# Four attention projections as 64x64 tiles in one round beside the scores, in a kernel of eight fused blocks

## The chip, the cores and the metric

The kernel is one program on one core of a Trainium2 chip. The time is device time in microseconds from launch to end, and each kernel is run several times. Five engines work from queues of their own, each in program order: TensorE (PE, with its weight loads shown apart as PEld), VectorE (DVE), ScalarE (ACT), GpSimd (POOL), and SyncE (SP), which issues DMAs. They wait for each other through semaphores.

## The reference

The input is 4096 tokens of 128 numbers. Four layers follow each other, each an attention block and a feed-forward block, each on the layer norm of what came before and added to it. The change lies in the last part, where layer 2 and layer 3 are computed together. Layer 2's attention has 16 heads of 64 numbers over sequences that the kernel treats in batches of 512 tokens:

```
def _L2_attn_ref(x, q_w, q_b, k_w, k_b, v_w, v_b, l_w, l_b):
    q = jnp.einsum('bsd,hpd->bhsp', x, q_w) + q_b
    k = jnp.einsum('bsd,hpd->bhsp', x, k_w) + k_b
    v = jnp.einsum('bsd,hpd->bhsp', x, v_w) + v_b
    scores = jnp.einsum('bhqp,bhkp->bhqk', q, k) / jnp.sqrt(jnp.float32(P))
    attn = jax.nn.softmax(scores, axis=2)
    ctx = jnp.einsum('bhqk,bhkp->bqhp', attn, v)
    out = concat @ l_w.T + l_b
```

The softmax runs over the queries (axis 2), so that each key has its own maximum and sum. Its four projections are q, k, v and the output projection with l_w. Layer 2's feed-forward is a mixture of experts on the first 1024 tokens. Layer 3's first block is a product with W1 plus a causal filter of 20 taps followed by a product with W2; its second block quantizes its inputs to a 4-bit grid in blocks of 16, takes a gate and an up product (352 wide), multiplies silu(gate) by up, quantizes again, and takes the down product.

## The kernel before

All tokens stay on the chip as eight tiles x[b] of 128 partitions by 4 x 128 (a batch b of 512 tokens). Layers 0 and 1 come first and are not touched by the diff. The function `late` (from L1386) does layers 2 and 3. Its main loop (L2140) has N = 64 *frames*, one for each batch b and pair of heads cc (n = 8 b + cc). The order on every engine is written out by hand: the program is recorded with a manual schedule, and each engine executes its instructions in the order in which the Python code emits them. A frame emits:

- `scores(n, 0)` (L1494): for two of the four key tiles, four products of 64 rows by 64 columns by 512, which use the four quarters of the PE array, into a buffer of two banks (`bank2`, two buffers); DVE takes the maxima (L1514), ACT the exponentials with sums (L1520).
- the hook "P", called between the exponentials of the two key tiles, then the hook "V".
- `context(n-1)` (L1542): sixteen records of 128 rows by 64 columns by 512, into the bank "c", copied to `ct` by ACT (L1555).
- `weigh(n, 0)` (L1530), which divides the values by the sums on DVE and POOL, and the hook "G".
- `scores(n, 1)` for the other two key tiles.
- `queries(n+2)` (L1482): two products of 128x128 by 512, to `pk` and `pq`; ACT evacuates q (L1490), DVE k (L1491).
- `output(n-1, ct)` (L1558): four products by token, `ct` as weights, l_w moving, 128 columns each, accumulated over the eight frames of a batch in the bank "o"; after the eighth DVE adds it to x[b] (L270).
- `values(n+1)` (L1465): four products by token into the bank "c"; DVE evacuates v (L1480).
- `weigh(n, 1)` and the hook "E".

The products are float32; each call of `mm` (L246) leaves two load and two matmul records in the trace. `bank()` without a name gives one of two buffers of one bank in turn ("one"), which queries share with everything that the hooks compute on PE.

Everything else is hung into the frames by a table: `at(frame, hook, f)` (L1404). The layer norm that prepares layer 2's input of batch b (`norm_steps`, L1412: `stats` on DVE and POOL, `scale` on ACT, `turn_`, four PE transposes and a copy by ACT) is hung in from frame 8 b - 10 (L1934). Two batches go through the experts after frames 9 and 17 (L1588). Layer 3 of batch b starts at frame 8 b + 8, or 8 b + 9 for b < 2 (L1940), and `planned` (L1884) hangs its steps into the frames after that: norm, filter taps on DVE (`conv_v`) and on ACT with POOL (`conv_s`), `conv_out` (two products and the addition), a second norm, `quant_x1`/`quant_x2`, `turn_x`, four times `gated` (gate and up on PE, tanh on ACT) with `gated_v` on DVE, `quant_h1`/`quant_h2`, `turn_h` and `down`. For b > 0 three of the four gated products stand in hook "E", and the queries of those frames are emitted earlier, between the second scores' exponentials (`early_q`). Layer 3 of the last batch, and the end of the one before it, are written out in `end` (L1961).

Of the kernel before, what the change touches and what calls it, by code (L numbers as in the profile page):

```python
# [17 lines left out]
F32 = mybir.dt.float32  # L18
I32 = mybir.dt.int32
U32 = mybir.dt.uint32  # L20
AF = mybir.ActivationFunctionType
ALU = mybir.AluOpType
AX = mybir.AxisListType

P = 128
D = 128
NB = 8
# [133 lines left out]
def body(ctx, tc, dram, spans, x_in, ib, it, ic, ei, out):  # L161
# [110 lines left out]
    def cols(t, j):  # L272
        return t[:, j * P : (j + 1) * P]
# [1112 lines left out]
    def late():  # L1386
# [11 lines left out]
        with tc.tile_pool(name="a2", bufs=2) as wp, tc.tile_pool(name="l3", bufs=1) as lp:  # L1398
            N = NB * 8
            qb = wp.tile([P, 8], F32, tag="qb", name="qb", bufs=1)  # L1400
            xts, vs_, qks, exs, outs = {}, {}, {}, {}, {}
            steps = {}

            def at(frame, hook, *fs):  # L1404
# [60 lines left out]
            def values(n):  # L1465
                if n < N:
                    b, cc = divmod(n, 8)
                    ps = bank("c")
                    pv = ps.rearrange("p (j n) -> p j n", j=J)
                    for j in range(J):  # L1470
                        mm(
                            pv[:, j, :],
                            cols(xts[b], j),
                            cols(a2["v"], cc),
                            start=(j == 0),
                            stop=(j == J - 1),
                        )
                    vs_[n] = v = wp.tile([P, J, P], F32, tag="v", name="v")
                    bias = cols(bc["vb"], cc).unsqueeze(1).to_broadcast([P, J, P])
                    nc.vector.tensor_tensor(v, pv, bias, ALU.add)  # L1480

            def queries(n):  # L1482
                if n < N:
                    b, cc = divmod(n, 8)
                    pk, pq = bank(), bank()
                    mm(pk, cols(a2["k"], cc), xts[b])
                    mm(pq, cols(a2["q"], cc), xts[b])
                    q = wp.tile([P, TB], F32, tag="q", name="q", bufs=3)
                    k = wp.tile([P, TB], F32, tag="k", name="k", bufs=3)
                    nc.scalar.activation(q, pq, AF.Identity, bias=qb[:, cc : cc + 1], scale=0.125)  # L1490
                    nc.vector.tensor_scalar(k, pk, a2["kb"][:, cc : cc + 1], None, ALU.add)  # L1491
                    qks[n] = q, k

            def scores(n, half, between):  # L1494


                q, k = qks[n]
                if half == 0:
                    ex = {}
                    sm = wp.tile([P, J, 2], F32, tag="sm", name="sm")  # L1500
                    vs = wp.tile([P, J, 2, 64], F32, tag="vs", name="vs")
                    exs[n] = ex, sm, vs
                ex, sm, vs = exs[n]
                tiles = (2 * half, 2 * half + 1)
                made = {}
                for kt in tiles:
                    ps = bank2()
                    for i in range(2):
                        r = slice(64 * i, 64 * (i + 1))
                        for m in range(2):  # L1510
                            at_ = kt * P + 64 * m
                            mm(ps[64 * m : 64 * (m + 1), i, :], k[r, at_ : at_ + 64], q[r, :])
                    nm = wp.tile([P, 2], F32, tag="nm", name="nm", bufs=4)
                    nc.vector.tensor_reduce(nm, ps, AX.X, ALU.max, negate=True)  # L1514
                    made[kt] = ps, nm
                for kt in tiles:
                    ps, nm = made[kt]
                    ex[kt] = wp.tile([P, 2, TB], F32, tag="ex", name="ex", bufs=7)
                    for i in range(2):
                        nc.scalar.activation(  # L1520
                            ex[kt][:, i, :],
                            ps[:, i, :],
                            AF.Exp,
                            bias=nm[:, i : i + 1],
                            accum_out=sm[:, kt, i : i + 1],
                        )
                    if kt == tiles[0]:
                        between()
# [350 lines left out]
                stats2, scale2, _, t2 = norm_steps(b, None, None, part)  # L1879
                return SimpleNamespace(**{k: v for k, v in locals().items() if callable(v)})  # L1880

            early_q = set()

            def planned(b, f0_):  # L1884

                s = layer3(b, *shared3(b))


                soon = b < 2 or b == NB - 2
                z = 9 - soon  # L1890
                plan = [
                    (1, "V", s.stats) if b < 2 else (0, "E", s.stats),
                    (1, "G", s.scale),
                    (1, "E", s.turn_),
                    (2, "V", lambda: s.conv_v(1, 2, 3, 4)),
                    (2, "G", lambda: s.conv_s(6, 7)),
                    (2, "E", lambda: s.conv_s(8, 9, 10)),
                    (2, "E", lambda: s.conv_v(5)),
                    (3, "G", lambda: s.conv_s(11, 12)),
                    (3, "E", lambda: s.conv_s(13, 14, 15)),  # L1900
                    (4, "G", lambda: s.conv_s(16, 17)),
                    (4, "E", lambda: s.conv_s(18, 19, 20)),
                    (5, "V", s.join),
                    (5, "E", s.conv_out),
                    (5, "E", s.stats2),
                    (6, "G", s.scale2),
                    (6, "E", s.quant_x1) if soon else (7, "V", s.quant_x1),
                    (z - 1, "V", s.quant_x2),
                    (z - 1, "E", s.turn_x),
                ]  # L1910
                for j in range(J):

                    if b > 0 and j > 0:
                        early_q.add(f0_ + z + j)
                        plan.append((z + j, "E", lambda j=j: s.gated(j)))
                        plan.append((z + j + 1, "V", lambda j=j: s.gated_v(j)))
                    else:
                        plan.append((z + j, "P", lambda j=j: s.gated(j)))
                        plan.append((z + j, "V", lambda j=j: s.gated_v(j)))
                plan += [  # L1920
                    (z + 2, "V", lambda: s.quant_h1(0)),
                    (z + 3, "V", lambda: s.quant_h2(0)),
                    (z + 4, "V", lambda: s.quant_h1(1)),
                    (z + 5, "V", lambda: s.quant_h2(1)),
                    (z + 5, "P", lambda: s.turn_h(0)),
                    (z + 6, "P", lambda: s.turn_h(1)),
                    (z + 6, "E", s.down),
                ]
                for frame, kind, f in plan:
                    at(f0_ + frame, kind, f)  # L1930
                return s


            for b in range(1, NB):  # L1934
                stats, scale, turn_, _ = norm_steps(b, new_xt(b), "lb")
                n = max(8 * b - 10, 3)
                at(n, "V", stats)
                at(n + 1, "G", scale)
                at(n + 1, "E", turn_)
# [21 lines left out]
            def end():  # L1961
# [3 lines left out]
                    layer3(NB - 1, xp, tile_, (2 * i, 2 * i + 2), "co"[i], "ge") for i in range(2)  # L1965
                )
                L = last
                f = start[NB - 2]
                for key in [k for k in steps if k[0] >= f + 8]:
                    del steps[key]  # L1970
                ct = context(N - 1)
                output(N - 1, ct)
                for h in (A, B):
# [162 lines left out]
            with tc.manual_schedule():  # L2136
                nc.vector.tensor_scalar(qb, a2["qb"], 0.125, None, ALU.mult)
                xts[0] = t[0]["next"]
                queries(0)
                for n in range(N):  # L2140
                    scores(n, 0, lambda: (n > 0 or (values(0), queries(1)), hook(n, "P")))
                    if n - 1 in experts_after:
                        waiting()
                    hook(n, "V")
                    if n - 1 in exs:
                        ct = context(n - 1)
                    weigh(n, 0)
                    hook(n, "G")
                    scores(n, 1, lambda: queries(n + 2) if n in early_q else None)
                    if n not in early_q:  # L2150
                        queries(n + 2)
                    if n > 0:
                        output(n - 1, ct)
                    values(n + 1)
                    weigh(n, 1)
                    hook(n, "E")
                    if n in experts_after:
                        eb, made = experts_after[n]
                        kept = []
                        waiting = experts(eb, made["xt"], lambda: kept.append(context(n)))  # L2160
                        ct = kept[0]
                end()
# [40 lines left out]
```

## Time and profile before

| | us |
|---|---|
| median of 3 runs | 1442.06 |
| lowest and highest | 1440.52, 1442.51 |
| the profiled execution | 1439.97 |
| span of its instructions | 1437.8 |

A profile page lists busy time by engine, then the chain of work that ended last, followed back from the end. A *group* is the instructions of one line, operation and shape; `ps<-q,k 64*64 64x512` are the scores (weights of 64 rows by 64 columns, 512 columns moving), `ps<-ex,vs` the context, `ps<-xt,blob_a` the queries, `ps<-blob_a,ct` the output projection and `ps<-blob_a,xt` the values. In a timeline line the first number is the start in us, the second how long the merged records last to the end of the last one, `xN` how many records there are, and the bracket what the engine waited for before. A matmul's recorded end lies after the start of the next, since they are pipelined; what a piece costs PE is therefore read from start to start.

The frames run from 505.97 us (frame 0) to 1370 us. Frame 9 starts at 606.88, frame 13 at 692.66, frame 17 at 740.25, frame 23 at 858.49, frame 25 at 887.18, frame 33 at 987.81, frame 49 at 1189.16.

### The profile page before, as it was taken

The page shows a single profiled execution, that of the slowest core. Times are in us where ns is not written, and L with a number is a line of the kernel's source. Part 1 is how long each engine was busy: PE and PEld are TensorE (multiplying, and loading weights), DVE is VectorE, ACT ScalarE, POOL GpSimd, SP SyncE. Part 2 cuts the span into 40 slices and gives each one's busy share as a digit, 9 for nine tenths or more (in the row PEclk, how much of TensorE's full clock was granted, in tenths as well). Part 3 has the DMA queues.
Part 4 walks back from the last instruction along what each step waited for, and adds up shares of the span by engine and source line. Part 5 has one row for each costly group of instructions (what it writes and reads, how often), then busy time and mean ns, then how long its engine had stood idle before and what let it go on. Part 6 is the DMA issues. An engine that isn't in the chain of part 4 may idle for free.

```text
span 1437.8 us, 24491 instructions
## 1 busy us (share of the span) xinstructions
PE 1378.9 (96%) x8838; PEld 644.4 (45%) x8838; DVE 984.5 (68%) x2072; ACT 1041.1 (72%) x2126; POOL 625.3 (43%) x726
## 2 busy tenths in 40 slices
PE   7889999999899999999999999999999999999997
PEld 3752222222377744434443444444454444444466
DVE  6776655676487877625671786786777877877876
ACT  7869999999887556656774676876867767768632
POOL 6747766666533523201620262442632633524423
PEclk9999999999999999999999999999999999999999
DMA  5039999899441010101000000000000000000000
GB/s 175 1 52 132 138 135 128 129 125 125 92 167 38 8 47 23 31 0 31 1 1 1 0 1 8 1 1 8 1 1 8 1 9 1 1 8 1 2 8 15
DMA packets 33241, 59.56 MB, mean 41 GB/s; under 512 B 5601, under 2 KB 25633, under 8 KB 28642
## 3 DMA queue, kind: packets, MB, share of 16 engines
q1 hardware_dynamic: 32416, 56.18, 22.1%
q8 instruction: 70, 1.15, 0.4%
q10 hardware_dynamic: 578, 1.57, 0.3%
q14 instruction: 49, 0.40, 0.1%
q0 software_dynamic: 128, 0.26, 0.1%
HBM read 49.70 MB, written 8.29 MB: 40 GB/s over the span
## 4 chain that ended last, share of the span: by engine, by line
PE 56%; DVE 4%; ACT 4%; issue 1%; POOL 0%; DMA 0%; DVEq 0%; ACTq 0%; POOLq 0%
PE ps L246 55%; ACT ex L1520 2%; DVE nm L1514 1%; ACT xn L1434 1%; PE ps L1850 1%; PE ps L1452 0%; DVE s L1422 0%; DVE fsc L1353 0%; DVE x L1756 0%; DVE fa L1358 0%; PE ps L1787 0%; DVE fa L1374 0%; DVE fa L1375 0%; DVE frc L1356 0%; DVE acc L1707 0%
## 5 line engine op out<-in xcount | busy, mean ns | idle before, releaser
L1520 ACT ACTIVATE ex<-ps,nm 128x512 f32<-128x512 f32 x512 | 345.6, 687 | 180.5 <-DVE nm L1514 178.6
L1514 DVE TENSOR_REDUCE nm<-ps 128x2 f32<-128x1024 f32 x256 | 300.4, 1215 | 57.0 <-PE ps L246 56.5
L246 PE MATMUL ps<-q,k 64*64 64x512 f32 x2048 | 251.4, 603 | 6.3 <-ACT ex L1520 5.3
L246 PE MATMUL ps<-ex,vs 128*64 128x512 f32 x1024 | 233.8, 598 | 0.0
L582 POOL TENSOR_TENSOR acc<-acc,pr 128x512 f32<-128x512 f32 x119 | 166.9, 1403 | 104.3 <-DVE pr L576 95.7
L1535 POOL TENSOR_TENSOR vs<-v,sm 128x256 f32<-128x256 f32 x128 | 81.3, 635 | 290.8 <-DVE sm L1534 261.5
L564 ACT ACTIVATE hm<-ps,blob_f 128x1536 f32<-128x1536 f32 x128 | 196.2, 1533 | 0.0
L246 PE MATMUL ps<-xt,blob_a 128*128 128x512 f32 x304 | 149.8, 618 | 1.3 <-issue 1.3
L576 DVE SCALAR_TENSOR_TENSOR pr<-ps,blob_f,gs 128x512 f32<-128x512 f32 x120 | 90.1, 751 | 88.5 <-PE ps L246 70.6
L246 PE MATMUL ps<-h,w 32*128 32x512 f32 x1024 | 147.4, 639 | 1.5 <-ACT hm L563 0.6
L246 PE MATMUL ps<-hm,w 128*32 128x512 f32 x1024 | 136.2, 604 | 2.0 <-DVE pr L576 2.0
L246 PEld LDWEIGHTS ps<-ex,vs 128*64 128x64 f32 x1024 | 67.8, 136 | 150.8 <-issue 129.7
L246 PEld LDWEIGHTS ps<-q,k 64*64 64x64 f32 x2048 | 64.2, 132 | 147.8 <-issue 66.0
L1722 POOL TENSOR_TENSOR acs<-acs,prod 128x512 f32<-128x512 f32 x98 | 124.7, 1272 | 10.5 <-ACT prod L1721 6.0
L242 POOL TENSOR_SCALAR rs<-mv 128x4 f32<-128x4 f32 (+1 forms) x69 | 17.9, 260 | 211.3 <-DVE mv L1424 140.5
L1520 ACT ACTIVATION_READ_ACCUMULATOR ex<-ps,nm 128x1 f32 x512 | 104.7, 205 | 0.0
L563 ACT ACTIVATE hm<-ps,blob_f 128x512 f32<-128x512 f32 x128 | 88.0, 687 | 17.5 <-PE ps L246 17.5
L246 PEld LDWEIGHTS ps<-xt,blob_a 128*128 128x128 f32 x304 | 52.4, 191 | 91.2 <-issue 61.3
L246 PEld LDWEIGHTS ps<-h,w 32*128 32x128 f32 x1024 | 40.7, 183 | 109.0 <-ACT hm L563 93.9
L1480 DVE TENSOR_TENSOR v<-ps,blob_bc 128x512 f32<-128x512 f32 x64 | 44.2, 691 | 66.0 <-PE ps L246 41.5
L246 PEld LDWEIGHTS ps<-blob_a,ct 128*128 128x128 f32 x512 | 67.0, 191 | 32.4 <-issue 29.2
L243 POOL TENSOR_TENSOR rs<-rs,half 128x4 f32<-128x4 f32 (+1 forms) x69 | 72.5, 1050 | 5.8
(310 smaller groups left out, 2163.2 us busy)
## 6 DMA issues: line engine op xcount, KB each, us to landing
gs<-gates SPq DMA_DIRECT2D x256, 128.0 KB
blob_f<-in_f SPq DMA_DIRECT2D x1, 2560.0 KB
blob_a<-in_a SPq DMA_DIRECT2D x1, 2056.0 KB
x<-in_x SPq DMA_DIRECT2D x8, 256.0 KB
gates<-eq SPq DMA_DIRECT2D x8, 256.0 KB
ge<-gates SPq DMA_DIRECT2D x4, 512.0 KB
back<-nought SPq DMA_DIRECT2D x7, 256.0 KB
by_rows<-fxn SPq DMA_DIRECT2D x7, 256.0 KB
```

The costliest lines, as they stand in the source:

```text
L242: nc.gpsimd.tensor_scalar(t, var, EPS, None, ALU.add)
L243: nc.gpsimd.tensor_tensor(t, t, half[:, : t.shape[-1]], ALU.pow)
L246: nc.tensor.matmul(out_, lhs, rhs, start=start, stop=stop)
L563: nc.scalar.activation(hm[:, 0, :], p1, AF.Gelu, bias=bias)
L564: nc.scalar.activation(hm[:, 1:, :], p3, AF.Gelu, bias=bias)
L576: nc.vector.scalar_tensor_tensor(pr, po, f0["b2"][:, e : e + 1], gs, ALU.add, ALU.mult)
L582: nc.gpsimd.tensor_tensor(acc[:, b, :], acc[:, b, :], pr, ALU.add)
L1480: nc.vector.tensor_tensor(v, pv, bias, ALU.add)
L1514: nc.vector.tensor_reduce(nm, ps, AX.X, ALU.max, negate=True)
L1520: nc.scalar.activation(ex[kt][:, i, :], ps[:, i, :], AF.Exp, bias=nm[:, i : i + 1], accum_out=sm[:, kt, i : i + 1],)
L1535: nc.gpsimd.tensor_tensor(vs[:, tiles, :, :], vs_[n][:, tiles, :].rearrange("p j (i n) -> p j i n", i=2), sm[:, tiles, :].unsqueeze(3).to_ ...
L1722: nc.gpsimd.tensor_tensor(t["acs"], t["acs"], p, ALU.add)
```

## The change

In frames 1 to 61 a new function `project` takes the place of `queries`, `output` and `values`. It computes the same four projections, but every product is cut into 64 rows by 64 columns, so that it runs in the tile shape of the scores. It has four phases. In each, one product uses the low 64 rows of the array and another the high 64 rows:

| phase | low rows | high rows |
|---|---|---|
| 1 | k (512 columns moving) | output (by token, 128 moving) |
| 2 | q (512 columns moving) | values (by token) |
| 3 | output | k |
| 4 | values | q |

Each product is thus accumulated over two phases, from two halves of the rows. A product's second half must not write its bank while the first half still does; `mark` puts a nop on SP that waits for the end of phase 1 (and 2), and the first matmul of phase 3 (and 4) waits for that nop. The evacuations of q, k and v come after all four phases.

The table is changed as well. `conv_out`, `turn_x` and all four `gated` stand in hook "P" (for the batch before the last, `conv_out` and `turn_x` stay in "E"), and `early_q` is gone. Layer 3 is one frame longer from the gated products on (z = 10, or 9 for b < 2; for the batch b = 5 the last steps are pulled forward again), `down` stands at z + 7 instead of z + 6, and the norm of layer 2's next batch is hung in from frame 8 b - 8 instead of 8 b - 10. One filter tap moves from frame 2's to frame 3's DVE work. The number of DVE and ACT instructions stays the same.

```
+            def project(n):
+                b, cc = divmod(n + 1, 8)
+                b2, cc2 = divmod(n + 2, 8)
+                bo, co = divmod(n - 1, 8)
+                pk, pq, pv = bank(), bank(), bank("c")
...
+                ct, xq, xv = cts.pop(n - 1), xts[b2], xts[b]
...
+                def mark(ins):
+                    m = nc.sync.nop(nofuse=True).ins
+                    tc.add_manual_dep(m, ins.name, SYNC)
+                    return m
...
+                one = mark(by_tokens(po, ct, wl, high, co == 0, False))
+                wide(pq, "q", low, True)
+                two = mark(by_tokens(pv, xv, wv, high, True, False))
+                after.append(one)
+                wide(pk, "k", high, False)
+                by_tokens(po, ct, wl, low, False, co == 7)
+                after.append(two)
+                wide(pq, "q", high, False)
+                by_tokens(pv, xv, wv, low, False, True)
+                queries_out(n + 2, pk, pq)
+                if co == 7:
+                    add_to_residual(bo, po)
+                values_out(n + 1, pv)
...
-                soon = b < 2 or b == NB - 2
-                z = 9 - soon
+                soon = b < 2
+                last_one = b == NB - 2
+                w = int(b == NB - 3)
+                z = 10 - soon
...
+                        (6, "P", s.conv_out),
+                        (6, "V", s.stats2),
+                        (6, "E", s.scale2),
+                        (7, "V", s.quant_x1),
+                        (7, "E", s.quant_x2) if soon else (8, "V", s.quant_x2),
+                        (z - 1, "P", s.turn_x),
+                    ]
+                    for j in range(J):
                         plan.append((z + j, "P", lambda j=j: s.gated(j)))
                         plan.append((z + j, "V", lambda j=j: s.gated_v(j)))
...
+                        (z + 5 - w, *"VE"[w], lambda: s.quant_h2(1)),
+                        (z + 5 - w, "P", lambda: s.turn_h(0)),
+                        (z + 6 - w, "P", lambda: s.turn_h(1)),
+                        (z + 7 - 2 * w, "E", s.down),
...
-                n = max(8 * b - 10, 3)
+                n = max(8 * b - 8, 3)
                 at(n, "V", stats)
                 at(n + 1, "G", scale)
                 at(n + 1, "E", turn_)
...
-                    scores(n, 1, lambda: queries(n + 2) if n in early_q else None)
-                    if n not in early_q:
+                    scores(n, 1)
+                    if 0 < n < N - 2:
+                        cts[n - 1] = ct
+                        project(n)
+                    else:
                         queries(n + 2)
-                    if n > 0:
-                        output(n - 1, ct)
-                    values(n + 1)
+                        if n > 0:
+                            output(n - 1, ct)
+                        values(n + 1)
```

## The prediction

> **What bounds the kernel now.** I read the page from the top: PE is busy for 96% of the span, and the chain that ended last runs over PE for 56%, nearly all of it on the helper line L246. I then asked for the busy time by stretch, because an average over five layers says little about the stretch that the diff touches.
>
> ```profile
> PE 1378.9 (96%) x8838; PEld 644.4 (45%) x8838; DVE 984.5 (68%) x2072; ACT 1041.1 (72%) x2126; POOL 625.3 (43%) x726
> ...
> PE 56%; DVE 4%; ACT 4%; issue 1%; POOL 0%; DMA 0%; DVEq 0%; ACTq 0%; POOLq 0%
> ```
> ```profile
> 900.00:1000.70 100.70, 100.70 (x629) 47.01 (x628) 77.57 (x133) 74.84 (x194) 41.09 (x48) 1.00 0.01 4
> ```
>
> The reader is to see that eight frames (one batch; the next two batches take the same) last 100.70 us and that PE is busy in all of it, at full granted clock, while DVE (77.6) and ACT (74.8) have room. So here a PE microsecond saved is a microsecond gained, as long as no queue takes it back. Then the PE timeline. Frame 13 (from 692.66) holds layer 2 alone; the starts tell what each piece costs:
>
> ```profile
> 692.66 1.95 PE L246 MATMUL ps<-q,k 64*64 64x512 f32 x16
> 694.54 3.65 PE L246 MATMUL ps<-ex,vs 128*64 128x512 f32 x16
> 698.12 1.95 PE L246 MATMUL ps<-q,k 64*64 64x512 f32 x16
> 700.00 1.98 PE L246 MATMUL ps<-xt,blob_a 128*128 128x512 f32 x4
> 701.82 1.05 PE L246 MATMUL ps<-blob_a,ct 128*128 128x128 f32 x8
> 702.71 1.06 PE L246 MATMUL ps<-blob_a,xt 128*128 128x128 f32 x8
> 703.70 1.95 PE L246 MATMUL ps<-q,k 64*64 64x512 f32 x16
> ```
>
> From start to start: scores 1.88, context 3.58, scores 1.88, queries 1.82, output 0.89, values 0.99; 11.04 in all. Each product is two records (float32 in two passes). Eight records of 128 columns take 0.89, so 128 columns stream in about 0.107 (plus 0.003 each) and 512 in 0.427. Four score tiles run side by side: 16 records are 4 x 0.427 = 1.71, and the row has 1.88, so 0.17 goes on changing the tile shape: about 0.11 to run empty (the values take 0.10 more before scores than the output before values) and 0.05 for a first load of 64 columns. A first load of 128 columns shows 0.11 (queries: 1.82 less 1.71). The frame changes shape four times.
>
> **The change, part by part** (from the profiled 1439.97 us, span 1437.8 and 2.2 around it; the median of the runs is 1442.06, 2.1 higher, and the answer is given on the median).
>
> *The round.* In frames 1 to 61 (61 of them) the four projections run as 64x64 tiles, the low rows on one product and the high rows on another, in four phases. A wide phase of a tile is 2 x 0.427 = 0.85; a phase by tokens is 8 x 0.1095 = 0.88. All four tiles work, so the round streams for 2 x 0.85 + 2 x 0.88 = 3.46, no less than now (1.71 + 2 x 0.88 = 3.46). What goes is the shape change on both sides. New frame: scores 1.71 + 0.11, context 3.58, scores 0.05 + 1.71, round 3.46: 10.62 against 11.04; I take 0.41 saved, **25.0** in 61 frames. No row of before shows such mixed rounds. Bounds: nothing exposed, as inside a score group (3.41), up to one first load exposed at each phase (4 x 0.05, so 3.66), which costs 12. I take the score rows, which are the nearest: the same tiles, loads and two passes. The waits through SP (a nop behind the first phase, waited for at the third) have the second phase as cover: 0.87 less 0.16 of tail (a 128-column record lasts 275 ns against 107 streamed), 0.7. SP has only DMA issues queued, and those of these frames wait for things done a frame earlier; past 0.7 the excess would be paid 61 times, with everything behind it on PE.
>
> [...]
>
> *Products moved to P*, between the first scores and the context. There 128x128 work enters and leaves by itself. Gate and up cost 0.70 + 0.68 in P and 0.59 + 0.58 in E (0.68 there holds an exit that the frame pays anyway):
>
> ```profile
> 1112.25 0.76 PE L246 MATMUL ps<-wt_gate,xt 128*128 128x352 f32 x2
> 1112.85 0.76 PE L246 MATMUL ps<-wt_up,xt 128*128 128x352 f32 x2
> 1113.53 0.66 PE L246 MATMUL ps<-q,k 64*64 64x512 f32 x4
> ```
> ```profile
> 1189.16 1.95 PE L246 MATMUL ps<-q,k 64*64 64x512 f32 x16
> 1191.04 0.86 PE L246 MATMUL ps<-wt_gate,xt 128*128 128x352 f32 x2
> 1191.73 0.76 PE L246 MATMUL ps<-wt_up,xt 128*128 128x352 f32 x2
> ```
>
> So 0.21 for each of 27 moved steps (15 gated, 6 conv_out, 6 turn_x): **-5.7**. *Steps left in E* followed 128x128 values; now they lie between the round and scores, both 64x64: leave 0.11, enter 0.11, leave 0.11, enter 0.05, about 0.40. Frames 2 to 6, 9, 10, 17, 18, 25, 33, 41, 49, 57 and 61: 15 x 0.40 = **-6.0**. Streams alone: 25.0 - 5.7 - 6.0 = 13.3 better.
>
> *What is late next.* Queries used to be evacuated while output and values ran (1.8 us). Now pq ends with the round, and `bank()` has two buffers. A lone turn_ in E takes pk's buffer, free by then. But norm steps two frames later put into one frame (25, 33, 41, 49) the turn_ of the next batch, `down` and layer 3's turn_, and both scales in G. `down` takes pq's buffer, so it waits for ACT's q, which stands behind eight scales and four exponentials. The rows:
>
> ```profile
> 1188.90 0.69 DVE L1480 TENSOR_TENSOR v<-ps,blob_bc 128x512 f32<-128x512 f32 x1 [0.27 <-PE ps L246]
> 1189.51 0.17 DVE L1534 RECIPROCAL sm<-sm 128x4 f32<-128x4 f32 x1
> 1189.59 0.84 DVE L1422 BATCH_NORM_STATS2 s<-x 128x6 f32<-128x128 f32 x4
> ```
> ```profile
> 723.06 3.20 ACT L1434 ACTIVATE xn<-x,nb,rs 128x128 f32<-128x128 f32 x8
> 726.14 0.69 ACT L1520 ACTIVATE ex<-ps,nm 128x512 f32<-128x512 f32 x1
> ```
>
> With T the start of such a frame: DVE evacuates k (0.61) and adds po (0.65) after phase three, then v, reciprocal and statistics (1.93 from start to end above), and takes its first maximum only at T+2.65. ACT: two exponentials (0.66 each, as in all rows of L1520) from T+3.87 to 5.2, the copy for turn_x to 5.7, two more to 7.0, ct to 7.5, eight scales (3.08 from start to start) to 10.6, tap weights 0.28 (frames 25 to 44), four exponentials (2.67) to 13.5, q to 14.1. PE: 1.82 + 0.65 + 3.58 + 1.77 + 0.1 + 3.46 ends the round at T+11.4 and the first turn_ at 12.06. `down` waits 2.05 (1.8 in frame 49): **-8.0**. Frames 9 and 17 have two turns and eight scales by the same chain, 0.9 each: **-1.8**. Frames 5 after a multiple of 8, where DVE has quant_h2 and the join (3.6 us): maxima 1 us late, second score bank 0.2 late, **-1**. Frames 18 and 19 wait for ACT and DVE now (their starts show 0.5 to 0.9 idle several times), so 0.41 gains nothing there: **-0.8**. In return frame 23 loses its wait, since `down` of batch 0 moves to frame 25; with what follows it **+1.9**:
>
> ```profile
> 870.24 0.60 PE L1452 MATMUL ps<-blob_c,xn 128*128 128x128 f32 x4
> 872.36 2.94 PE L246 MATMUL ps<-wd,ht 128*128 128x128 f32 x24 [1.52 <-ACT q L1490]
> ```
>
> That row is also the nearest to the new wait: `down` behind q, 1.52. Sum: 13.3 - 8.0 - 1.8 - 1 - 0.8 + 1.9 = 3.6 better. From the median: 1442.06 - 3.6, so **1438.5 us**. A measurement of this kernel tells about 0.2% (2.9 us) from no change.
>
> **Rivals.** *The queues give way*: if q is free by the first turn_ (maxima or scales earlier than in my chain), the 8.0 stays: 1430.5. For it: DVE and ACT have a quarter of their time free. Against: the row at 872.36. *Rounds lose at their phase changes* (the slower side): the next phase's first load and the return of the SP nop are not hidden, 0.2 per round, 12 in all: 1450.7. Nothing in before shows 80 matmuls with 80 loads in 3.5 us; the densest rows have one pair per 0.107. It turns my gain into a loss from 0.06 per round and shows as slower from 0.11. *The halves do not overlap*, so that the change doesn't do what it says: 3.46 more per round, 1442 + 208 = 1650. Against it the score rows.
>
> **The numbers.** Forecast 0.50 (1431 to 1445 by its own bounds: of it 0.27 faster, 0.20 same, 0.03 slower); queues give way 0.18, all faster; phase changes 0.27 (0.01 of it same); no overlap 0.05. Together faster 0.45, same 0.21, slower 0.34. The range reaches from a little below the second case, 1428, to 1455, which takes in 3.66 per round with the waits as counted; it leaves out the last case and the outer part of the others.
>
> **What would show it.** Right: the round from its first record to the next scores in 3.4 to 3.5 us, scores after it in 1.82, a frame without other work near 10.6; `down` in frames 25, 33, 41 and 49 idle about 2 us behind ACT q L1498; eight frames near 101. Wrong: a round of 3.7 or more, a wait for SP within it, no idle time at `down`, or idle time at the gates in P.

## The result and the profile after

The changed kernel is slower: a median of 1464.31 us in six runs (1459.11 to 1467.80) against 1442.68 in six runs of the kernel before (1440.52 to 1446.43). The ratio is 1.0144, with a 95% interval of 1.0118 to 1.0170. The prediction had 1438.5 with a range of 1428 to 1455, so a gain of 3.6; measured is a loss of 21.6. The profiled run of the changed kernel is its shortest: 1459.11, span 1457.3, mean granted clock 0.992 where the kernel before had 1.000.

The first thing to compare is what the prediction rested on, the round. The PE timeline of the changed kernel, frame 13 from its first scores to those of frame 14 (columns: start, length from first start to last end, engine, line, operation, tiles, shape, number of records):

```profile
692.98 1.90 PE L247 MATMUL ps<-q,k 64*64 64x512 f32 x16
694.81 3.65 PE L247 MATMUL ps<-ex,vs 128*64 128x512 f32 x16
698.39 1.95 PE L247 MATMUL ps<-q,k 64*64 64x512 f32 x16
700.16 0.59 PE L1517 MATMUL ps<-xt,blob_a 64*64 64x512 f32 x2
700.17 0.60 PE L1517 MATMUL ps<-blob_a,ct 64*64 64x128 f32 x8
700.59 0.59 PE L1517 MATMUL ps<-xt,blob_a 64*64 64x512 f32 x2
700.61 0.60 PE L1517 MATMUL ps<-blob_a,ct 64*64 64x128 f32 x8
...
703.62 0.61 PE L247 MATMUL ps<-q,k 64*64 64x512 f32 x4
```

Two records of 512 columns and eight of 128 start within 0.02 us of each other: the row halves do run side by side. The round takes 703.62 - 700.16 = 3.46 us, the scores before and after it 1.77 and 1.83, the frame 10.64 against 11.04. The step that looked riskiest was right: 0.40 saved per frame, where 0.41 was predicted. The time went somewhere else, and the PE waits between 500 and 1400 us name the place (columns: who waits, for whom, us in total, times, longest):

```profile
PE ps L247 <- ACT q L1498: 7.2, 5, 1.8
PE ps L1862 <- POOL fa L1377: 6.6, 2, 3.3
PE ps L247 <- ACT ex L1595: 5.7, 16, 1.1
PE ps L1925 <- POOL h L1377: 3.8, 1, 3.8
```

Of the first row 6.4 us are the predicted wait of `down` for q. The second and the fourth have no counterpart before, and no term of the prediction stands for them: the transposition `turn_x` (L1862, frames 17 and 25) and `turn_h` (L1925, frame 63) stand and wait for the last instruction of a rounding (L1377). What such a wait costs beyond itself is seen in the timeline around it, here frame 17 with all engines, and in the busy time of the stretch before the turn and of the stretch from it (columns: PE, PEld, DVE, ACT, POOL busy, granted clock, DMA):

```profile
741.59 1.06 POOL L1377 TENSOR_TENSOR fa<-fa,fsc 128x512 f32<-128x512 f32 x1 [1.88 <-DVE fa L1376]
742.67 0.69 ACT L1595 ACTIVATE ex<-ps,nm 128x512 f32<-128x512 f32 x1 [4.23 <-POOL fa L1377]
742.70 0.71 PEld L1862 LDWEIGHTS ps<-blob_c,fa 128*128 128x128 f32 x4 [4.16 <-POOL fa L1377]
742.70 1.11 PE L1862 MATMUL ps<-blob_c,fa 128*128 128x128 f32 x4 [3.27 <-POOL fa L1377]
```
```profile
739.00:742.50 3.50, 0.42 (x4) 0.00 (x0) 3.40 (x6) 0.00 (x0) 1.62 (x2) 1.00 0.00 0
742.50:746.00 3.50, 3.30 (x10) 1.49 (x12) 2.45 (x12) 3.27 (x9) 1.21 (x3) 0.51 0.00 0
```

PE stands idle for 3.27 us, and when it starts again its clock is granted at 0.51 for the next 3.5 us: the turn takes 1.04 instead of 0.59, the context behind it 4.65 instead of 3.58. Nearly the same happens in frame 25 (3.28 idle, then 0.46 and 0.93 too long). It is worst in frame 63, whose context takes 5.69 (1389.05 - 1383.36):

```profile
1381.88 1.54 PE L1925 MATMUL ps<-blob_c,h 128*128 128x128 f32 x6 [3.77 <-POOL h L1377]
1383.36 5.76 PE L247 MATMUL ps<-ex,vs 128*64 128x512 f32 x16
1389.05 1.52 PE L247 MATMUL ps<-q,k 64*64 64x512 f32 x12
```

To compare kernels below I use, besides the median, the *stretch*: from the start of the first context to the start of the last, by the PE timeline of the profiled run. It is 857.13 us before (518.54 to 1375.67) and 875.50 after (519.63 to 1395.13): 18.4 longer. What lies ahead of it, layers 0 and 1, is the same code in every kernel here, yet its length varied by 0 to 10 us from one profiled run to the next, with pieces at a lowered clock in changing places (in the changed kernel 0.50 from 83.75 to 87.15 us); the medians contain that, the stretch does not.

Where the stretch grew, against the predicted 3.6 shorter: the two turns of x with their slow clock, 4.8 + 4.7; the turn of h, where 3.77 + 0.68 + 2.11 is 6.6 in place, of which 5.9 reach the length of frames 62 and 63; `down` of frame 33, which ran at half clock after its wait (4.41 instead of the 2.78 of frame 41), 1.6. These are 17.0 us. Against them stands that `down` waited 6.4 in all and not the 8.0 predicted. So of the 22.0 by which the prediction missed some 6.6 are left: 1.6 is a wait of conv_out for ACT's copy of ht in frame 23, and about 5 are spread over the frames. I did not take these apart one by one.

### The profile page after: what moved, and what is told of

Read it like the earlier page. It is cut to its first block, busy times and chain, and to the rows that moved or that the text cites. A ratio compares the mean times of both kernels' runs of the same rounds, so it can differ in the third digit from the quotient of the medians.

```text
span 1457.3 us, 31939 instructions
## 1 busy us (share of the span) xinstructions
PE 1378.7 (95%) x12498; PEld 708.4 (49%) x12498; DVE 991.0 (68%) x2072; ACT 1041.7 (71%) x2126; POOL 623.0 (43%) x726
## 3 DMA queue, kind: packets, MB, share of 16 engines
q10 hardware_dynamic: 578, 1.57, 0.3%
## 4 chain that ended last, share of the span: by engine, by line
PE 57%; ACT 23%; DVE 14%; issue 2%; DMA 2%; POOL 2%; SPq 1%; DVEq 0%; POOLq 0%; ACTq 0%
PE ps L247 45%; PE ps L1517 10%; ACT hm L565 8%; ACT ex L1595 5%; ACT hm L564 4%; DVE nm L1589 2%; ACT xn L1435 2%; DMA gs<-gates 1%; DVE fa L1375 1%; DVE fa L1376 1%; DVE s L723 1%; ACT h L385 1%; ACT prod L1796 1%; DVE fm L1374 1%; ACT q L1498 1%
## 5 line engine op out<-in xcount | busy, mean ns | idle before, releaser
L247 PE MATMUL ps<-ex,vs 128*64 128x512 f32 x1024 | 237.9, 607 | 0.0
L1517 PE MATMUL ps<-xt,blob_a 64*64 64x512 f32 x976 | 222.2, 589 | 0.0
L247 PEld LDWEIGHTS ps<-q,k 64*64 64x64 f32 x2048 | 69.4, 132 | 141.0 <-issue 87.5
L1797 POOL TENSOR_TENSOR acs<-acs,prod 128x512 f32<-128x512 f32 x98 | 125.3, 1279 | 11.6 <-ACT prod L1796 7.2
L1517 PE MATMUL ps<-blob_a,xt 64*64 64x128 f32 x1952 | 126.9, 269 | 0.0
L1517 PE MATMUL ps<-blob_a,ct 64*64 64x128 f32 x1952 | 126.9, 269 | 0.0
L1517 PEld LDWEIGHTS ps<-blob_a,ct 64*64 64x64 f32 x1952 | 113.7, 133 | 0.0
L1517 PEld LDWEIGHTS ps<-blob_a,xt 64*64 64x64 f32 x1952 | 110.3, 133 | 0.0
```

The lines of the kernel that those rows point to most:

```text
L247: nc.tensor.matmul(out_, lhs, rhs, start=start, stop=stop)
L1517: ins = nc.tensor.matmul(*args, **kw).ins
L1797: nc.gpsimd.tensor_tensor(t["acs"], t["acs"], p, ALU.add)
```

## The experiments

The theory after the result: **the plan, not the round, costs**. In three places (x of batches 0 and 1, h of batch 5) it puts a rounding into hook E and its turn into hook P of the next frame, so that PE has only the first scores, 1.8 us, between them; PE waits 3.3 to 3.8 us, and the idle time then lowers its clock. The rivals: **the density of the rounds lowers the clock** (80 loads in 3.5 us), and **the longer program is fetched late** (99 packets on the queue of instructions against 70). In the table every median stands beside the ratio to the kernel before on the same chip (its medians there were 1441.4 to 1444.6).

| kernel | median us | ratio, 95% interval | stretch us |
|---|---|---|---|
| before | 1442.68 | 1 | 857.1 |
| changed | 1464.31 | 1.0144 (1.0118 to 1.0170) | 875.5 |
| e1 turn of x in E | 1457.91 | 1.0112 (1.0083 to 1.0142) | 871.7 |
| e2 rounding of h earlier | 1461.18 | 1.0106 (1.0072 to 1.0140) | 872.8 |
| e3 `down` first | 1453.67 | 1.0065 (1.0040 to 1.0091) | 868.5 |
| e4 all three | 1447.74 | 1.0024 (1.0008 to 1.0041) | 859.1 |
| e5 e4, rounding of x in V | 1440.41 | 0.9983 (0.9967 to 1.0000) | 854.0 |
| e6 changed, waits filled | 1457.04 | 1.0111 (1.0083 to 1.0138) | 868.8 |
| e7 rounds on the old plan | 1446.78 | 1.0029 (1.0013 to 1.0044) | 861.2 |
| e8 new plan, no rounds | 1471.65 | 1.0207 (1.0181 to 1.0233) | 882.1 |
| e9 e5, three steps in P | 1442.21 | 0.9999 (0.9984 to 1.0013) | 858.6 |
| e10 e7, gates in P | 1440.24 | 0.9979 (0.9960 to 0.9997) | 853.1 |
| e11 e10, `down` first, conv_out in P | 1456.92 | 1.0095 (1.0074 to 1.0115) | 869.0 |
| e12 e10, `down` first | 1434.65 | 0.9946 (0.9928 to 0.9964) | 849.8 |

**e1: the turn of x half a frame later.**

```
-(z - 1, "P", s.turn_x),
+(z - 1, "PE"[soon], s.turn_x),
```

> Edit: batches 0 and 1 turn their rounded x in hook E of frames 17 and 25, where 128x128 work stands anyway, and no longer half a frame earlier, in P. Theory (the moved turn stands too close behind its rounding): the profiled run of the changed kernel has PE idle for 3.27 and 3.28 us before these two turns, with the turn at 1.04 and 1.05 instead of 0.59 and the context behind it at 4.65 and 4.59 instead of 3.58, as the granted clock falls after the idle time. All of it goes: 4.8 + 4.7, and the turn costs no change of shape in P (0.2 each), so about 9.5 to 10 off a median of 1464.3: 1454.5, and no idle time over 1 us ahead of either turn; frames 17 and 25 gain one turn in E (0.5, part of it in the existing waits). Rival (the rounds with their 80 loads lower the granted clock, idle time or not): only the idle time comes back, 6.5, so 1458, and the contexts of frames 17 and 25 stay above 4.5. Second rival (a longer program, fetched late: 99 packets on the queue of instructions against 70): the wait moves with the turn, 1464.

Less than half of it came: the stretch is 3.8 shorter, not 9.5. The median, 1457.91, is the number of the first rival (1458), but not by its mechanism: the contexts of frames 17 and 25 run at full speed again (3.65 from first start to last end, where that rival had them above 4.5). The waits ahead of both turns are gone, and the stretches from context to context that held them (those of frames 16 and 24, from here on counted from the context in the frame to the one in the next) are 4.4 shorter each. But frames 17 and 25 became 1.2 and 3.6 longer. The wait had hidden something else: the rounding stands in DVE's queue in front of the first maxima of frame 25, so that the exponentials come late and the second scores wait for their bank, 2.4 us behind ACT ex, with a granted clock of 0.90 and 0.93 in the 20 us from 880 on. While the turn waited, this was hidden beneath it. The rounding had to move as well (e5).

**e2: the rounding of h half a frame earlier.**

```
-(z + 4, "V", lambda: s.quant_h1(1)),
-(z + 5 - w, *"VE"[w], lambda: s.quant_h2(1)),
+(z + 4 - w, "VE"[w], lambda: s.quant_h1(1)),
+(z + 5 - w, "V", lambda: s.quant_h2(1)),
```

> Edit: batch 5 scales its second pair of h one hook earlier (frame 61, E) and rounds it in V of frame 62 instead of E, so that turn_h of frame 63 has a frame between it and its rounding. Theory (too close behind its rounding): in the profiled run of the changed kernel PE is idle for 3.77 us before this turn, the turn takes 1.48 instead of 0.8 and the context behind it 5.7 instead of 3.58: 6.5 goes, less up to 1 that VectorE pays in frames 61 and 62 where the maxima come later, so 1458 to 1459. Rival (rounds lower the clock): only 3.8 comes back, 1460.5, the context of frame 63 stays above 5; frames 62 and 63 hold no round, which speaks against this rival from the start. Second rival (late instructions): 1464.

The wait of 3.8 is gone, and from frame 62 to the end the profiled run is 4.5 us better, which is more than the 3.8 of the wait alone and less than the 5.5 to 6.5 expected; 1.4 us stay in frame 62, of which 1.1 is a wait of its second scores for ACT ex. The stretch as a whole is only 2.7 shorter, because frame 17 had its half clock for 6.8 us in this run, where it was 3.4 in the changed kernel. The median does not settle it (3.1 off, with runs from 1454.6 to 1465.2).

**e3: `down` ahead of the turns in hook E.**

```
+if f is s.down:
+    steps.setdefault((f0_ + frame, kind), []).insert(0, f)
+else:
     at(f0_ + frame, kind, f)
```

> Edit: in hook E `down` comes ahead of the turn_ steps, so that it takes the buffer that k left and the first turn_ takes the one of q, 2.8 us later. Theory (the wait for q as predicted): `down` waits for q in frames 25, 33, 41 and 49 (7.2 us over 5 waits in the profiled run, the longest 1.81), and after one of them the clock fell (`down` of frame 33 took 4.41 instead of 2.78): 7 to 9 goes, 1455.5 to 1457.5, no wait for ACT q at `down`. Rival (the round's evacuation is late by more than that, so that k's buffer is no better): under 2 off, 1463, and `down` waits for DVE k instead.

As expected by the stretch, which is 7.0 shorter; the median fell by more, 10.6. Of the 7.0, 1.6 is the half clock of frame 33. Of the waits for q one of 0.8 is left, and in its place there are four short ones behind the evacuation of `down` itself, at most 0.3 each. One buffer was free early and one late; the step that needed its buffer first had got the late one.

**e4: all three.** The edits of e1, e2 and e3 together.

> All three edits together. Theory: they are independent, so 9.7 + 6 + 8 come off 1464.3: about 1440.5, with the granted clock at 1.00 from 500 us to the end; that is about 2 below the kernel before. Rival (rounds lower the clock): 6.5 + 3.8 + 7 off, 1447, clock still below 1.00 in places. Second rival (longer program): 1455 or more.

The stretch is 16.4 shorter, the granted clock is 1.00 in every 10 us from 520 to 1440, and the median is 1447.74: 7 above the theory, and at the first rival's 1447. The number does not decide for that rival, since its clock part is wrong: with the waits gone the rounds run at full clock. Of the missing 7 us e5 finds 5: they are what e1 had uncovered.

**e5: the rounding of x behind the first maxima.** For batches 0 and 1, beyond e4:

```
-(7, "E", s.quant_x2) if soon else (8, "V", s.quant_x2),
+(8, "V", s.quant_x2),
```

> All three edits, and the rounding of x of batches 0 and 1 stands in V of frames 17 and 25 (behind the first maxima) instead of E of frames 16 and 24 (ahead of them). With the three edits alone the second scores of frame 25 waited 2.43 us for ACT ex, because VectorE did rounding and statistics (2.5 and 1.4 us) ahead of the first maxima. Theory (the rounding delays whatever stands next in VectorE's queue): the wait of 2.43 goes, frame 25 takes about 2.5 less, frame 17 about 1 less; the stretch from the first context to the last goes from 859.1 (three edits; before: 857.1) to 855.5, the median from 1447.7 to about 1444. Rival (the wait is for ScalarE's own queue, not the maxima): no change, 1447.7.

The rival falls: frame 25 is 2.5 us shorter and frame 17 2.3, the stretch 854.0, the median 1440.41. So the changed kernel's idea with its plan mended is no slower than the kernel before and 24 us faster than the changed kernel, with the same 12498 matmul records.

**e6: the waits stay, but PE has something to do.** The filling is the kernel's own helper `keep_clock`, which it calls in other parts too: products of the identity with itself, into a buffer that nobody reads.

```
+*([(z - 1, "P", lambda: keep_clock(12))] if soon else []),
 (z - 1, "P", s.turn_x),
...
+*([(z + 6 - w, "P", lambda: keep_clock(14))] if w else []),
 (z + 6 - w, "P", lambda: s.turn_h(1)),
```

> The changed kernel with 12 transposing-size products of the identity (2.6 us) ahead of turn_x in frames 17 and 25, and 14 (3.0 us) ahead of the second turn_h in frame 63, so that TensorE has work in the three long waits; nothing is taken from the waits themselves. Theory (idle time lowers the granted clock, which then doubles the next 1.5 to 2.8 us): the three turns and the contexts behind them run at 0.59, 0.59, 0.8 and 3.58; 1.5 + 1.5 + 2.8 = 5.8 off the stretch from first to last context (875.5 to about 869.7), the median at 1458.5; the idle time ahead of the turns shrinks to under 1 us but the turns start at the same distance from their frames' start. Rival (the density of the rounds lowers the clock): more work makes it no better, 875 or more, 1464.

This separates the wait from the clock. The PE timeline of e6 at frame 63 (28 filling records, then the turn and the context):

```profile
1373.20 3.39 PE L247 MATMUL ps<-blob_c 128*128 128x128 f32 x28
1377.04 0.87 PE L1925 MATMUL ps<-blob_c,h 128*128 128x128 f32 x6 [0.45 <-POOL h L1377]
1377.85 3.65 PE L247 MATMUL ps<-ex,vs 128*64 128x512 f32 x16
1381.43 1.09 PE L247 MATMUL ps<-q,k 64*64 64x512 f32 x8
```

The turn still starts when POOL has rounded, but it takes 0.81 and the context 3.58 (1381.43 - 1377.85), where the changed kernel had 1.48 and 5.69. The stretch is 6.7 shorter (expected 5.8), but 1.6 of that lies in frame 33, where nothing was filled: the wait of `down` there is as long as before (1.80), and this time no half clock followed. The three filled places account for 4.9. More work made the kernel faster there, with the rounds as they were, so it was the idle time and not the rounds' density that lowered the clock in these three places. (The second rival, late instructions, falls with e5 and e12, which have 99 packets of instructions and none of the loss, and with e8, which has the waits without a single round.)

**e7 and e8: the rounds without the plan, the plan without the rounds.** e7 takes `planned` and the norm steps of the kernel before; e8 replaces the condition `if 0 < n < N - 2:` by `if False:`, so that queries, output and values are emitted as before.

> The rounds of the changed kernel with the plan of the kernel before (gates, conv_out and turn_x in E, norm steps two frames earlier, queries never ahead). Theory (rounds gain 0.41 each, and each E frame gives 0.40 back): 25.0 less some 46 E frames at 0.40 (18.4), less 0.35 in each of 15 gated frames where `up` takes the buffer that q leaves late (5.2): 1440 to 1443, and no idle time of 3 us anywhere. Rival (the rounds themselves cost what the trace of the changed kernel lost): 1455 or more, with a lower clock in many frames.

> The plan of the changed kernel with the queries, output and values of the kernel before, without rounds. Theory (the plan, not the rounds, costs): the three waits with their clock (9.5 + 6.5), `down` behind q (6 to 8 with a lowered clock), 27 steps in P (5.7), less 1.9 in frame 23: 1442 + 27 = about 1469, idle times of 3 us ahead of turn_x in frames 17 and 25 and of turn_h in frame 63. Rival (rounds cost, plan neutral): 1442 to 1450, waits ahead of the turns under 1.5.

e8 is the clearest single answer: the plan alone costs 24.9 us of stretch, and it has the same three waits (2.8 us at most at L1862, 3.8 at L1925). Frame 17 of e8 has the half clock as well, for 3.4 us from 749.07 on, without a single round in the kernel:

```profile
749.58 1.12 PE L1862 MATMUL ps<-blob_c,fa 128*128 128x128 f32 x4 [2.77 <-POOL fa L1377]
750.63 4.55 PE L247 MATMUL ps<-ex,vs 128*64 128x512 f32 x16
```

Put on this plan, the rounds gain 6.6. e7 shows the other half: on the old plan the rounds gain nothing. The stretch got 4.0 longer, where I expected 1.4 shorter. I take it that the gates and products in E cut the rounds off from the scores, and that a visit to E costs more than I had priced; e10 tests this for the gates.

**e9: three steps of E into P.** On e5: `down` and both turns of frames 25, 33, 41 and 49, and the `down` and turn of 57, go to P of the frame behind; there `down` comes first and layer 3's turn second.

```
-(1, "E", s.turn_),
+(1, "E", s.turn_) if soon else (2, "P", s.turn_),
-(z + 7 - 2 * w, "E", s.down),
+(z + 5, "E", s.down) if w else (z + 8, "P", s.down),
-at(n + 1, "E", turn_)
+at(*((n + 2, "P") if b > 3 else (n + 1, "E")), turn_)
```

> The kernel with x rounded in V, and in frames 25, 33, 41, 49 and 57 the three steps of hook E (`down`, the turn of the next batch, layer 3's turn) go to P of the frame behind, where gates stand anyway. Theory (a visit of 128x128 work between round and scores costs its changes of shape, 0.40, and with the queues' lateness frame 41 there costs 1.3 more than the same steps cost before): 0.7 to 1.3 for each of five visits, 3.5 to 6.5 off the stretch from first to last context: 854.0 to about 849, the median from 1440.4 to about 1435.5. Rival (the turn of layer 3 now comes too late for the taps that read it in V of the same frame, so VectorE stands still and the second maxima are late): 854 or more, and a wait of PE for ACT ex over 1 us in frames 26, 34, 42, 50.

My theory fell: 4.5 longer, not 5 shorter. The rival's price came, but not by its mechanism. In the timeline of e9, frame 42:

```profile
1095.30 1.09 PE L247 MATMUL ps<-q,k 64*64 64x512 f32 x8 [0.61 <-ACT ex L1595]
1095.70 0.21 ACT L1595 ACTIVATION_READ_ACCUMULATOR ex<-ps,nm 128x1 f32 x1
1095.80 0.69 ACT L1595 ACTIVATE ex<-ps,nm 128x512 f32<-128x512 f32 x1
1096.37 0.22 ACT L1595 ACTIVATION_READ_ACCUMULATOR ex<-ps,nm 128x1 f32 x1
1096.46 0.70 ACT L1498 ACTIVATE q<-ps,qb 128x512 f32<-128x512 f32 x1
...
1096.63 1.09 PE L247 MATMUL ps<-q,k 64*64 64x512 f32 x8 [0.24 <-ACT ex L1595]
```

In these frames ACT works on eight scales for 3.1 us just ahead of the exponentials. The three steps in E had kept PE busy for that time. Without them the first scores of the next frame come at once, wait for the exponentials that hold their banks, and split into two groups of eight records, so that the way from the context of frame 41 to that of frame 42 takes 1.2 us longer than in e5. I read this as follows: what stood in E was a cover.

**e10: the old plan, and only the gates moved.**

```
-if b > 0 and j > 0:
-    early_q.add(f0_ + z + j)
-    plan.append((z + j, "E", lambda j=j: s.gated(j)))
-    plan.append((z + j + 1, "V", lambda j=j: s.gated_v(j)))
...
+late_ = int(b > 0 and j > 0)
+plan.append((z + j + late_, "P", lambda j=j: s.gated(j)))
+plan.append((z + j + late_, "V", lambda j=j: s.gated_v(j)))
```

> The rounds on the plan of the kernel before, with one thing moved: the 15 gate steps go from E to P of the next frame, half a frame, and every rounding keeps its distance to its turn. Theory (per gate step 0.40 for the E visit and 0.24 for the wait of `up` for q go, 0.21 for P comes): 15 x 0.43 = 6.4 off the stretch of the round-alone kernel, 861.2 to 854.7; median 1446.8 to about 1440.5. Rival (the gates in P delay the context and with it the queues): 859 or more, PE waits for ACT ex over 9 us in all.

As expected and a little better: the 15 steps bring 8.1, so 0.54 each and not 0.43. This is the part of the changed plan that the round needs, without the part that hurts.

**e11: conv_out in P as well, and `down` first.**

```
-(5, "E", s.conv_out),
-(5, "E", s.stats2),
+(5, "E", s.conv_out) if b == NB - 2 else (6, "P", s.conv_out),
+(5, "E", s.stats2) if b == NB - 2 else (6, "V", s.stats2),
```

> The kernel of the previous line with `down` ahead of the turn in E, and conv_out of batches 0 to 5 from E to P of the next frame (its statistics in V there). Theory: 0.2 for each of six conv_out steps, and up to 0.6 for each of some five waits of `down` for q: 2 to 4 off 854.7, 851 to 852.5; median 1437 to 1438.5. Rival (statistics half a frame later make the rounding of x late for its turn in E): idle time ahead of L1862 of over 1 us, 855 or more.

Its stretch is 16 longer than that of e10, and 19 longer than that of e12 below, from which it differs in these lines alone. The waits between 500 and 1400 us in e11:

```profile
PE ps L247 <- ACT ex L1595: 14.4, 22, 2.4
PE ps L247 <- ACT ht L1931: 6.9, 5, 1.4
```

Neither is the one my rival named, though both come from the move. In P, conv_out stands right behind a `turn_h`, whose buffers ACT must first copy (the second row). In V, the statistics now stand in the same frame as a rounding: an addition, two statistics and the rounding keep DVE from 1056.0 to 1062.2 in frame 38, the scales wait for them, the exponentials for the scales, and the scores for those (2.36, 2.35 and 2.06 us in three batches, the last two with a lowered clock behind them, 0.87 and 0.83 in the 10 us from 1060 and from 1170). The changed kernel has these steps in different frames, since it moves the chain from the gates on by one frame and the next batch's norm by two; in that rearrangement the roundings of batches 0, 1 and 5 lost their distance.

**e12: e10 and `down` first.** The edit of e3 on e10.

> The rounds on the plan before with the gates in P (the kernel whose first-to-last-context stretch was 853.05), and `down` ahead of the turns in hook E, nothing else. Theory (the only wait for q of over 1 us left in that kernel is `down` of batch 0 in frame 23, 1.5 us, behind the first turn; with k's buffer it needs no wait): 1.5 to 2 off, 851.2 to 851.6, median 1438.5, about 3 below the kernel before. Rival (the turn behind `down` then waits for q as long, or the first maxima of frame 24 come later): 852.7 to 853.3, median 1440.

The best of all: 1434.65, ratio 0.9946 (0.9928 to 0.9964), the stretch 7.3 shorter than before, and 3.2 shorter than in e10, of which 1.8 in frame 23 as expected; 0.35 to 0.43 each in four later frames was not expected. The waits in e12 are back to a list like that of the kernel before:

```profile
PE ps L247 <- ACT ex L1595: 5.5, 12, 1.1
PE ps L247 <- DVE cg L1697: 1.6, 2, 0.8
```

## Why the prediction was wrong, step by step

- **The round: right.** Predicted 3.46 per round and 0.41 saved; measured 3.46 and 0.40. The rival "rounds lose at their phase changes" (0.2 per round) and "the halves do not overlap" are out, and no wait of PE for SP's nops appears. In the output's rows of before, records of 128 columns start every 0.11 us with a load of 0.19 us each; in the round's, records by token on the same rows of the array start every 0.11 us with a load of 0.13 us each, so the loads ran beside the matmuls. The records by token start at 700.17, ahead of the second pair of wide ones at 700.59, which the program emits first.
- **"Products moved to P", 0.21 for each of 27 steps: the step that failed.** The price of the change of shape is right (frames 42 to 44 hold one moved gate each and came out 0.40 - 0.20 shorter). But it was the only price I gave. For each of the 27 steps I asked what it costs on PE and not when its input is ready, so the wait of a turn for its rounding stood in the sum at nothing. The diff also moves three roundings later (quant_x2 of batches 0 and 1 to E of the frame ahead of its turn in P, quant_h2 of batch 5 the same), and the working has no line for them. Three such places cost 4.8, 4.7 and 5.9, 15.4 us with the clock. The rows were at hand: in the kernel before, the rounding of batch 1's x starts on DVE at 880.14, POOL ends it at 883.68, and the turn comes at 886.65, 3 us later.

```profile
880.14 0.42 DVE L1370 TENSOR_SCALAR fm<-fa 128x512 int32<-128x512 int32 x1
...
882.62 1.06 POOL L1376 TENSOR_TENSOR fa<-fa,fsc 128x512 f32<-128x512 f32 x1 [5.35 <-DVE sm L1534]
...
886.65 0.60 PE L1787 MATMUL ps<-blob_c,fa 128*128 128x128 f32 x4
```

- **The clock: an assumption that was not written down.** The sum held the granted clock at 1.00 because every window of before shows 1.00, though with idle times of at most 1.5 us there. The price of a wait was taken as the wait; after 3.3 us it was nearly one and a half times that (4.8 for 3.27), after 3.77 it was 5.9 (e6 shows the difference to be the clock).
- **`down` behind q, 2.05, 2.05, 2.05 and 1.8: right in place and mechanism, somewhat large in size.** Measured 1.25, 1.81, 1.80 and 1.51 in frames 25, 33, 41 and 49; e3 removes them by swapping buffers, as the chain in the prediction suggests. The half clock behind the one in frame 33 was not in it.
- **Frames 9 and 17, 0.9 each: right** (0.96 each, turn_ behind ACT q). **Frame 23, 1.9 better: gone again**, as conv_out, moved to P, waits there for ACT ht (1.57): once more a moved step whose producer was not looked up.
- **"Streams alone 13.3 better": too good.** e5 has none of the long waits and is 3.1 better than before; the prediction without its 8.0 for `down` comes to 11.6. In a batch like that of frames 41 to 48, frames 45 and 47 gain nothing from the round, since the scores at their end wait for exponentials: frame 47 holds the same pieces on PE as frame 46 and takes 12.20, where that one takes 11.45. So PE was not the bound there. And a step in E costs more than the shape changes at 0.40 (e10: 0.54 + 0.21 saved for each step that leaves it, waits of `up` for q included).
- **The rivals.** None of my rivals had the mechanism: on the slower side I put a fault in the round, because the round was new, and none in the plan, which is the other half of the diff.

## What to carry to other kernels

When a plan is rearranged, list for every moved step its producer's last instruction and the instant at which its new place comes up, not only what it costs on its engine; a step that only changes place by half a frame can lose the distance that hid a chain of four instructions on DVE and one on POOL, 3.5 us long. Where TensorE waits as long as in the three places here, count more than the wait: 3.27 us cost 4.8, and 3.77 cost 5.9. And a stretch of work that looks like a detour may be the cover for a late engine: before taking it away, ask what the next step waits for.

## What the runs showed of the hardware

- Late in a wait or just behind it the granted clock fell to half for 3.4 us (in frame 17 of the changed kernel from 742.51 to 745.93; in frame 63 for 6.8), and records of 128 columns started every 0.213 us instead of 0.11 (`down` of frame 33). Two waits of equal length in one run of the changed kernel, in frames 33 and 41, had different ends; `down` took 4.41 us in the first and 2.78 in the second:

```profile
1005.19 4.57 PE L247 MATMUL ps<-wd,ht 128*128 128x128 f32 x24 [1.81 <-ACT q L1498]
...
1109.34 2.94 PE L247 MATMUL ps<-wd,ht 128*128 128x128 f32 x24 [1.80 <-ACT q L1498]
```

- In the stretches of the fourteen profiles all ten waits of PE of 3.27 to 3.77 us had a half clock with them (three each in the changed kernel and in e3, two in e2, one each in e1 and e8), seven of the fifteen from 1.79 to 2.8 us, and none of those under 1.7. In the stretch no half clock came without such a wait, in kernels with rounds or without. Of the eight waits of 1.8 us three had one, in the changed kernel, e1 and e2; what told these from the other five was not shown.
- 38 products that nobody reads, some 8 us of PE work put into three waits, made these three places 4.9 us shorter (e6).
